# Bias rows, single weight loads, a second batch in plain fp32 and a new order in an attention and feed-forward block

## The chip, the cores and the metric

The kernel runs on one core of one Trainium2 chip. The core has five instruction streams that matter here: TensorE (PE, with its weight loads PEld), VectorE (DVE), ScalarE (ACT), GpSimd (POOL) and SyncE (SP), which issues most of the DMA transfers. The metric is the time of one execution on the device in microseconds, as the median of several runs. The profile is of one more execution, with times from the start of its span.

## The reference

For each of 16 batches of 512 tokens with 256 features, in fp32: linear attention with 16 heads of 16, a residual and a layernorm, then a feed-forward layer with ternary weights, a residual and a layernorm.

```
q, k, v = x @ Wq.T + bq, x @ Wk.T + bk, x @ Wv.T + bv       # by heads of 16
qe, ke  = exp(q - max(q)), exp(k - max(k))                    # max over the 16 of a head
kv      = ke.T @ v                                            # 16 x 16 of each head
y       = (qe @ kv) / (qe . sum(ke) + 1e-6)
x1      = layernorm(x + y @ Wo.T + bo)
Wt      = clip(round(W / (mean|W| + 1e-5)), -1, 1)            # for W1 and W2
out     = layernorm(x1 + relu(x1 @ Wt1.T + b1) @ Wt2.T + b2)
```

## The kernel before

**The work of a batch.** A batch is four tiles of 128 tokens. The stages, by the names of the steps (a number behind a name is the tile, the half or the chunk):

- `ldt`, `ldx` load x turned (features on partitions) and x as it is. `xt`, `xtl` split the turned x into a high part in the fp32r type and the low rest.
- `qk` (L680) multiplies a tile by the q and k weights, 512 columns, in three products per chunk of 128 features: high by high, high by low, low by high. Batch 0 uses plain fp32 instead (`qkF`, L670). `mxa` (L690) adds the bias from the tile `bqk`, which holds the same row in all partitions, `mxb` (L696) takes the maximum of each head, `mxs` (L700) subtracts it, `ex` (L711, L713) takes the exponential, for k a second time into fp32r.
- `ks`, `ksh`, `ksl`, `pks` (L758) sum exp(k) over the tokens. `dena` (L762), `denb`, `denc`, `nrm` (L790) divide exp(q) by its denominator, giving `qs`.
- `g` (L813, plain fp32 in batch 0: `gF`, L809) multiplies x by exp(k); `ge` copies it; `kv` (L840) multiplies it by the v weights `wv`; `kvm`, `kvb`, `kvp`, `kvh`, `kvl` mask and split it; `m` (L868) folds in the output weights.
- `qs` has to be turned. Batch 0 does it on TensorE (`qt`, L941, with `qteF` copying it out of PSUM). Batches 1 to 15 use a 32 x 32 transpose on VectorE (`qtr`, L898), a write to DRAM (`qtw`, L905), four reads back (`qtd`, L912), and `qtbe`, `qtbl` for the split.
- `o` (L1066, plain in batch 0: `oF`, L1062) gives the attention's output, `or` (L988) adds it to x. `xb` (L823) has added `bo` to x before. `nm`, `nq`, `nv`, `np`, `na` are the layernorm. `x1b` (L1081) adds `b2` for later.
- x1 is turned in the same two ways (`xt1...`): on TensorE in batches 0 and 15.
- `f` (L1098) is the first layer, eight chunks of 128 of the 1024 inner features, with `ha` (relu, L1104), `hc` and `hb` (the split of the result); `z` (L1135) is the second layer; `zr`, `ym`, `yq`, `yv`, `yp`, `ya` add, take the layernorm, and `st` stores. In the last batch the second layer is cut by tiles (`zL`) and each tile has its own layernorm, so that stores start early.

**The start.** `lqk0`, `lqk1` load the q and k weights in two halves of the features, by ACT's queue; `wh`, `wl` split them. `lbqk` loads the two biases into `bqk`, each read 128 times from DRAM, once per partition. `lw0` and `lw1` load the four pieces each of W1 and W2, `sa0` and `sa1` sum their absolute values, `tot`, `half` make the threshold, `qn` and `qz` (L580) make each piece ternary. `lvo` loads, one behind the other, `bv`, `wv`, `wo`, `bo` (repeated to all partitions), `b1` and `b2` (repeated). `warm0` and `warm1` are products of ones with ones on TensorE whose results nobody reads, twelve and two of them.

**The order.** No loop runs at build time in the order of the stages. A table `ORDER` gives each step of each batch a number, all steps are sorted by it, and each engine executes its own instructions strictly in that order. `OTHER` lists the steps and batches that use the second of two possible engines (for instance `mxs` on VectorE instead of GpSimd).

```
order = [(ORDER[name][0], 0, name, fn) for name, fn in startup_steps()]
for b in range(NB):
    order += [(ORDER[name][b], b, name, fn) for name, fn in steps(b)]
for _, b, name, fn in sorted(order, key=lambda e: e[0]):
    ...
```

So a step that waits holds up everything behind it on its engine, and a transfer that waits holds up everything behind it on SP. Buffers are few: two for the turned x (`xt32`), one for `ex`, two PSUM banks for each of four groups of uses (`qk` and the transposes; `g`, `kv`, `m`, `o`, `pks`; `f`; `z`). `GB` and `OB` say how many of the first batches use the plain form for `g` and for `o`; `MOVED` says which batches turn `qs` and x1 by way of DRAM; `WARM` holds the numbers of warm-up products.

Of the kernel before, what the change touches and what calls it, by code (L numbers as in the profile page):

```python
# [17 lines left out]
F32 = mybir.dt.float32  # L18
F32R = mybir.dt.float32r
AF = mybir.ActivationFunctionType  # L20
# [23 lines left out]
GB = 1  # L44
OB = 1
KB = 0
JB = 2
MOVED = {"qt": range(1, 16), "xt1": range(1, 15)}
WARM = (12, 2)
GROUPS = {"s": 2, ("y", 15): 4, ("s", 15): 4}  # L50
OTHER = {
    "xtl1": (1, 3, 7, 15),
    "qn2": (0,),
    "ks": (0, 1, 2, 4, 5, 8, 11),
    "ksl": (0, 1, 2, 3, 4, 5, 7, 8, 10, 11, 12, 13, 14, 15),
    "qn0": (0,),
    "xsl1": (1, 3, 12, 13),
    "qn1": (0,),
    "qn3": (0,),
    "mxs0": (1, 9, 10, 11, 12, 13, 14),  # L60
    "qn6": (0,),
    "nm0": (0, 1, 2, 3, 5, 7, 8, 9, 10, 11, 14),
    "ek0": (1, 3, 4, 8, 9, 10, 11, 12, 13, 14),
    "ek1": (1, 2, 3, 4, 6, 7, 8, 9, 11, 12, 13, 14, 15),
    "nv0": (0, 3, 8, 9, 13),
    "kvp": (1, 3, 4, 5, 7, 9, 12, 14, 15),
    "xb0": (1, 3, 7, 12, 15),
    "kvl": (1, 2, 3, 4, 5, 7, 8, 10, 11, 12, 13, 15),
    "xsl0": (2, 4),
    "xb1": (1, 3, 4, 13),  # L70
    "qn7": (0,),
    "qn4": (0,),
    "x1b1": (0, 6, 11),
    "qn5": (0,),
    "qtbl0": (2, 3, 4, 9, 15),
    "x1b0": (0, 1, 7, 9, 11, 12, 13),
    "xt1bl0": (1, 2, 3, 5, 7, 10, 14),
    "hc4": (1, 5, 6, 9, 14),
    "nrm0": (3, 7, 8, 9, 10, 11),
    "na0": (2, 6, 8, 14),  # L80
    "mxs1": (4, 7, 13, 14),
    "mxs2": (4, 7, 13, 14, 15),
    "xt1bl1": (2, 3, 4, 5, 6, 10, 12),
    "ym0": (1, 2, 5, 8),
    "na2": (3, 4, 15),
    "hc5": (2, 7, 13, 14, 15),
    "hc7": (2, 5, 10, 11, 12, 13, 15),
    "qtbl1": (4, 7, 15),
    "yv0": (2, 3, 4, 6, 11),
    "nrm1": (5, 11, 13, 14),  # L90
    "ya0": (2, 6, 7, 8, 12, 13, 15),
    "na1": (4, 7, 11, 14, 15),
    "mxs3": (7, 10, 13),
    "hc2": (4, 5, 6, 8, 11, 13, 14),
    "hc3": (4, 12, 13, 14),
    "ya3": (3, 6, 11, 12, 13),
    "hc6": (4, 8, 9),
    "xtl0": (10, 13),
    "hc1": (5, 7, 10, 11, 12, 15),
    "ya2": (4, 11, 13, 14, 15),  # L100
    "ya1": (5, 7, 11, 12, 13, 14),
    "hc0": (9, 10, 13, 14),
    "na3": (10, 13),
    "ym2": (15,),
    "yv1": (15,),
    "yv2": (15,),
    "ym3": (15,),
# [4 lines left out]
    "warm0": (2,),  # L112
    "wh0": (3,),
    "ldt0a": (4, 0, 0, 0, 0, 0, 0, 0, 0, 0, 0, 0, 0, 0, 0, 0),
    "qkF0_0": (5, 0, 0, 0, 0, 0, 0, 0, 0, 0, 0, 0, 0, 0, 0, 0),
    "wl0": (6,),
    "ldt1a": (7, 0, 0, 0, 0, 0, 0, 0, 0, 0, 0, 0, 0, 0, 0, 0),
    "wh1": (8,),
    "wl1": (9,),
    "lbqk": (10,),  # L120
    "qkF0_1": (11, 0, 0, 0, 0, 0, 0, 0, 0, 0, 0, 0, 0, 0, 0, 0),
    "mxa0": (12, 101, 119, 271, 362, 547, 589, 741, 927, 1135, 1172, 1344, 1546, 1661, 1766, 1938),
    "ldt0": (0, 13, 61, 158, 231, 346, 335, 545, 743, 893, 792, 1025, 1049, 1380, 1562, 1505),
    "xt0": (0, 14, 62, 177, 257, 386, 387, 643, 809, 894, 831, 1113, 1220, 1402, 1644, 1808),
    "mxb0": (15, 113, 120, 279, 365, 550, 598, 744, 932, 1169, 1173, 1345, 1547, 1662, 1783, 1976),
    "ldt1": (0, 16, 72, 108, 208, 221, 411, 416, 690, 915, 826, 1099, 1082, 1363, 1631, 1725),
    "xt1": (0, 17, 77, 117, 239, 344, 467, 630, 775, 916, 901, 1231, 1218, 1392, 1657, 1847),
    "xtl1": (0, 18, 94, 141, 248, 402, 516, 634, 817, 933, 1024, 1249, 1219, 1393, 1705, 1848),
    "qkF1_0": (19, 0, 0, 0, 0, 0, 0, 0, 0, 0, 0, 0, 0, 0, 0, 0),
    "ldt1b": (20, 0, 0, 0, 0, 0, 0, 0, 0, 0, 0, 0, 0, 0, 0, 0),  # L130
    "mxs0": (21, 115, 155, 306, 420, 551, 662, 784, 961, 1170, 1326, 1401, 1548, 1672, 1826, 2008),
    "exF0": (22, 0, 0, 0, 0, 0, 0, 0, 0, 0, 0, 0, 0, 0, 0, 0),
    "ldt0b": (23, 0, 0, 0, 0, 0, 0, 0, 0, 0, 0, 0, 0, 0, 0, 0),
    "xtl0": (0, 24, 69, 183, 278, 413, 521, 659, 816, 945, 975, 1296, 1351, 1403, 1666, 1814),
    "qkF1_1": (25, 0, 0, 0, 0, 0, 0, 0, 0, 0, 0, 0, 0, 0, 0, 0),
    "mxa1": (26, 88, 160, 232, 322, 474, 670, 765, 871, 1053, 1184, 1394, 1452, 1680, 1840, 1903),
    "mxb1": (27, 89, 164, 244, 323, 514, 712, 799, 889, 1067, 1281, 1408, 1453, 1681, 1841, 1914),
    "lw0": (28,),
    "sa0": (29,),
    "mxs1": (30, 114, 165, 280, 446, 515, 730, 840, 953, 1100, 1300, 1409, 1511, 1728, 1842, 1990),  # L140
    "exF1": (31, 0, 0, 0, 0, 0, 0, 0, 0, 0, 0, 0, 0, 0, 0, 0),
    "lvo": (32,),
    "woh": (33,),
    "qkF2_0": (34, 0, 0, 0, 0, 0, 0, 0, 0, 0, 0, 0, 0, 0, 0, 0),
    "qkF2_1": (35, 0, 0, 0, 0, 0, 0, 0, 0, 0, 0, 0, 0, 0, 0, 0),
    "mxa2": (36, 58, 162, 205, 444, 472, 625, 783, 973, 1045, 1294, 1333, 1561, 1599, 1732, 1942),
    "mxb2": (37, 59, 185, 302, 447, 541, 626, 791, 974, 1107, 1305, 1334, 1563, 1605, 1733, 2004),
    "ldx": (38, 70, 179, 154, 326, 524, 642, 845, 931, 1076, 1269, 1386, 1556, 1706, 1717, 1948),
    "mxs2": (39, 71, 186, 327, 448, 564, 692, 847, 985, 1144, 1329, 1404, 1580, 1614, 1734, 2055),
    "exF2": (40, 0, 0, 0, 0, 0, 0, 0, 0, 0, 0, 0, 0, 0, 0, 0),  # L150
    "qkF3_0": (41, 0, 0, 0, 0, 0, 0, 0, 0, 0, 0, 0, 0, 0, 0, 0),
    "qkF3_1": (42, 0, 0, 0, 0, 0, 0, 0, 0, 0, 0, 0, 0, 0, 0, 0),
    "mxa3": (43, 50, 189, 291, 397, 609, 717, 824, 850, 1087, 1239, 1423, 1494, 1578, 1739, 2018),
    "mxb3": (44, 96, 190, 292, 401, 610, 718, 825, 851, 1102, 1274, 1424, 1545, 1583, 1825, 2019),
    "mxs3": (45, 106, 206, 330, 423, 611, 742, 844, 1011, 1121, 1278, 1435, 1569, 1633, 1845, 2020),
    "exF3": (46, 0, 0, 0, 0, 0, 0, 0, 0, 0, 0, 0, 0, 0, 0, 0),
    "sr0": (47,),
    "qk3": (0, 48, 188, 270, 376, 562, 716, 732, 839, 1073, 1205, 1310, 1442, 1577, 1738, 2007),
    "tot0": (49,),
    "half0": (51,),  # L160
    "qn2": (52,),
    "qk2": (0, 53, 161, 204, 366, 460, 607, 780, 856, 997, 1191, 1297, 1462, 1595, 1731, 1917),
    "wol": (54,),
    "ks": (55, 124, 214, 371, 478, 640, 746, 863, 1058, 1200, 1347, 1482, 1584, 1747, 1901, 2076),
    "ksh": (56, 128, 215, 372, 502, 653, 757, 885, 1060, 1201, 1356, 1483, 1601, 1758, 1915, 2102),
    "bvm": (57,),
    "gF0": (60, 0, 0, 0, 0, 0, 0, 0, 0, 0, 0, 0, 0, 0, 0, 0),
    "warm1": (63,),
    "ksl": (64, 133, 227, 382, 503, 654, 758, 890, 1061, 1204, 1367, 1496, 1602, 1759, 1926, 2122),
    "pks": (65, 148, 228, 383, 530, 677, 769, 913, 1095, 1208, 1368, 1497, 1606, 1773, 1943, 2123),  # L170
    "dena": (66, 149, 238, 384, 531, 678, 771, 922, 1096, 1211, 1369, 1500, 1616, 1775, 1944, 2124),
# [1055 lines left out]
```

## Time and profile before

| | us |
|---|---|
| median of 3 runs (484.08 to 484.88) | 484.31 |
| the profiled execution, whole | 484.78 |
| the profiled execution, its span | 483.1 |
| TensorE busy | 469.2 |
| VectorE busy | 439.9 |
| ScalarE busy | 406.2 |
| GpSimd busy | 378.8 |
| first product of `f` of batch 0 starts at | 47.93 |
| last product of TensorE starts at | 476.94 |

A busy time is the time in which an engine executes an instruction; register and semaphore instructions do not count. Products are pipelined, so the distance from one start to the next says more than a product's own length: 24 products of 128x256 in 2.87 us are 0.12 us apart, though each is listed with 0.28. Where a line names two engines around an arrow, the second ended the wait of the first. SP shows only the issue of a transfer; its landing is later by some microseconds, which the part on DMA issues gives as a median per line.

### The profile page before, as it was taken

How to read it: one execution, taken by the hardware profiler on the slowest of the kernel's cores; microseconds unless marked ns; L12 is line 12 of the kernel's file. 1: busy time of each engine (PE TensorE's matmuls, PEld its weight loads, DVE VectorE, ACT ScalarE, POOL GpSimd, SP SyncE). 2: the span in 40 equal slices, each digit the busy share in tenths (PEclk: the TensorE clock that was granted, in tenths of full speed). 3: DMA queues.
4: the chain of work that ended last, by engine and by line, in shares of the span. 5: the costliest groups of instructions: out<-in, count | busy, mean ns of one | idle time of the engine just before them, and what ended most of it. 6: DMA issues, size and time to landing. Idle time of an engine off the chain costs nothing.

```text
span 483.1 us, 9025 instructions
## 1 busy us (share of the span) xinstructions
PE 469.2 (97%) x2976; PEld 415.9 (86%) x2976; DVE 439.9 (91%) x859; ACT 406.2 (84%) x923; POOL 378.8 (78%) x391
## 2 busy tenths in 40 slices
PE   8989999999999999999999999999999999999995
PEld 5567899899888998989989898889989898898984
DVE  2889999999999999999999998999999988998964
ACT  3897998998889788997987989688898979966774
POOL 1788898976958999896989799798898778744524
PEclk9999999999999999999999999999999999999999
DMA  6931325071542745345332605323445145124102
GB/s 227 309 140 43 89 88 196 24 229 55 160 125 68 216 143 153 104 127 175 130 133 87 199 22 188 118 99 121 152 130 148 51 156 150 44 89 132 44 1 88
DMA packets 36671, 59.84 MB, mean 124 GB/s; under 512 B 4240, under 2 KB 22672, under 8 KB 36624
## 3 DMA queue, kind: packets, MB, share of 16 engines
q1 hardware_dynamic: 36048, 58.74, 38.1%
q8 instruction: 23, 0.38, 0.3%
q10 hardware_dynamic: 576, 0.52, 0.3%
q14 instruction: 24, 0.20, 0.2%
HBM read 35.66 MB, written 23.59 MB: 123 GB/s over the span
## 4 chain that ended last, share of the span: by engine, by line
PE 79%; DVE 6%; POOL 5%; DMA 4%; ACT 3%; issue 2%; ACTq 0%; POOLq 0%; DVEq 0%
PE ph L1098 22%; PE pz L1135 21%; PE pqk L680 14%; PE po L1066 8%; PE pg L813 8%; PE pkv L840 2%; PE pm L868 2%; DMA w32qk<-in_wkT_dram 1%; DMA x<-in_x_dram 1%; POOL qk L700 1%; DMA w<-in_w1T_dram 1%; DVE x1b L1037 1%; PE pg L809 1%; PE pks L758 1%; POOL rstd_z L1020 1%
## 5 line engine op out<-in xcount | busy, mean ns | idle before, releaser
L1104 ACT ACTIVATE ph<-ph,b_sb 128x512 f32<-128x512 f32 x128 | 83.7, 657 | 20.9 <-PE ph L1098 19.9
L700 POOL TENSOR_TENSOR qk<-qk,mx 128x512 f32<-128x512 f32 x45 | 51.6, 1150 | 12.7 <-DVE mx L696 12.1
L690 DVE TENSOR_TENSOR qk<-pqk,bqk 128x512 f32<-128x512 f32 x64 | 43.2, 679 | 3.8 <-PE pqk L680 1.5
L696 DVE TENSOR_REDUCE mx<-qk 128x32 f32<-128x512 f32 x64 | 43.4, 679 | 1.2
L711 ACT ACTIVATE ex<-qk 128x512 f32<-128x512 f32 x64 | 40.4, 631 | 3.9 <-POOL qk L700 3.1
L790 POOL TENSOR_TENSOR qs<-ex,rden 128x512 f32<-128x512 f32 x22 | 26.2, 1204 | 13.2 <-DVE rden L782 13.1
L1005 ACT ACTIVATE junk_z<-x1b,nm_z 128x256 f32<-128x256 f32 x64 | 32.2, 505 | 2.4 <-POOL nm_z L999 2.2
L1035 ACT ACTIVATE x<-x,nmr_o,rstd_o 128x256 f32<-128x256 f32 x50 | 28.0, 600 | 7.3 <-POOL nmr_o L1022 7.3
L1005 ACT ACTIVATE junk_o<-x,nm_o 128x256 f32<-128x256 f32 x64 | 32.1, 503 | 0.4
L823 POOL TENSOR_TENSOR x<-x,bo_bc 128x512 f32<-128x512 f32 x23 | 30.6, 1335 | 0.1
L1081 POOL TENSOR_TENSOR x1b<-x,b_bc 128x512 f32<-128x512 f32 x22 | 29.5, 1346 | 1.4 <-ACT x L1035 1.4
L988 DVE SCALAR_TENSOR_TENSOR x1b<-pz,x1b 128x256 f32<-128x256 f32 x64 | 24.7, 417 | 1.7 <-PE pz L1135 1.5
L988 DVE SCALAR_TENSOR_TENSOR x<-po,x 128x256 f32<-128x256 f32 x64 | 24.3, 417 | 1.5 <-PE po L1066 1.0
L1035 ACT ACTIVATE x1b<-x1b,nmr_z,rstd_z 128x256 f32<-128x256 f32 x39 | 21.8, 598 | 4.2 <-POOL nmr_z L1022 4.2
L777 DVE TENSOR_REDUCE den<-dent 128x64 f32<-128x1088 f32 x16 | 20.5, 1281 | 0.2
L762 DVE TENSOR_TENSOR dent<-ex,pks 128x1024 f32<-128x1024 f32 x16 | 19.4, 1214 | 1.0 <-PE pks L758 1.0
L898 DVE STREAM_TRANSPOSE rqT<-qs 128x1024 f32<-128x1024 f32 x15 | 18.6, 1240 | 1.7 <-POOL qs L790 1.3
L1020 POOL TENSOR_TENSOR rstd_z<-var_z,expo 128x4 f32<-128x4 f32 (+1 forms) x19 | 19.2, 1011 | 1.0
L898 DVE STREAM_TRANSPOSE rx1T<-x 128x1024 f32<-128x1024 f32 x14 | 17.4, 1240 | 1.9 <-ACT x L1035 1.2
L1020 POOL TENSOR_TENSOR rstd_o<-var_o,expo 128x4 f32<-128x4 f32 x16 | 18.1, 1131 | 0.8
L840 PEld LDWEIGHTS pkv<-g,wv 128*128 128x128 f32 x128 | 16.2, 191 | 2.2 <-ACT g L832 1.3
L840 PE MATMUL pkv<-g,wv 128*128 128x128 f32 x128 | 17.0, 276 | 0.7 <-ACT g L832 0.7
(899 smaller groups left out, 2122.6 us busy)
## 6 DMA issues: line engine op xcount, KB each, us to landing
x<-in_x_dram SPq DMA_DIRECT2D x16, 512.0 KB, 4.5
xt<-in_xT_dram SPq DMA_DIRECT2D x30, 256.0 KB, 4.1
wqT<-rqT SPq DMA_DIRECT2D x15, 512.0 KB, 2.6
dqT<-wqT SPq DMA_DIRECT2D x60, 128.0 KB, 3.2
out_dram<-x1b SPq DMA_DIRECT2D x30, 256.0 KB, 2.2
wx1T<-rx1T SPq DMA_DIRECT2D x14, 512.0 KB, 2.6
dx1T<-wx1T SPq DMA_DIRECT2D x56, 128.0 KB, 3.2
w<-in_w1T_dram SPq DMA_DIRECT2D x4, 256.0 KB, 4.2
```

The costliest lines, as they stand in the source:

```text
L680: nc.tensor.matmul(s.pqk[t], s.xt[i][:, c, tt], wqk[j][:, c, :], start=(c == 0 and n == 0), stop=(c == EC - 1 and n == 2))
L690: nc.vector.tensor_tensor(s.qk[t].rearrange("p g d -> p (g d)"), s.pqk[t], bqk, ALU.add)
L696: nc.vector.tensor_reduce(s.mx[t], s.qk[t], AX.X, ALU.max)
L700: engine(f"mxs{t}", b, nc.gpsimd, nc.vector).tensor_tensor(s.qk[t], s.qk[t], s.mx[t].unsqueeze(2).to_broadcast([P, 2 * NH, HD]), ALU.subtract)
L840: nc.tensor.matmul(s.pkv[:, cc], wv[:, ec, cc], s.g[:, ec, cc], start=(ec == 0), stop=(ec == EC - 1))
L988: nc.vector.scalar_tensor_tensor(out=r, in0=p[t], scalar=1.0, in1=r, op0=ALU.mult, op1=ALU.add, accum_out=stat("sum")[:, t:t + 1])
L1005: nc.scalar.activation(junk, getattr(s, what)[:, t, :], AF.Square, bias=n.nm[:, t:t + 1], accum_out=stat("sq")[:, t:t + 1])
L1020: nc.gpsimd.tensor_tensor(stat("rstd")[:, sl], n.var[:, sl], expo[:, sl], ALU.pow)
L1035: nc.scalar.activation(r, r, AF.Identity, bias=nmr, scale=rstd)
L1098: nc.tensor.matmul(s.ph[f], w1[:, c, f * P:(f + 1) * P], s.x1T[i][:, c, :], start=(n == 0), stop=(n == 2 * EC - 1))
L1104: nc.scalar.activation(s.ph[f], s.ph[f], AF.Relu, bias=b1_sb[:, f:f + 1])
L1135: nc.tensor.matmul(s.pz[t], hx[:, t * P:(t + 1) * P], w2[:, f, :], start=(done[tt] == 1 and t == tt[0] and i == 0), stop=(done[tt] == FC a ...
```

## The change

Four things change together.

1. The biases of q and k are loaded as one row each, 1 KB, into partition 0 of `bqk`, which is cleared before. `pbqk` multiplies a 128x128 tile of ones by it on TensorE, which puts the row into all partitions of a PSUM bank of the `qk` group, and `bqke` copies it back to `bqk` on ScalarE.
2. `lvo`, `lw0`, `lw1`, `sa0`, `sa1` are cut into steps of one instruction each (`lbv`, `lwv`, `lwo`, `lbo`, `lb1`, `lb2`, `lw0_0` to `lw1_3`, `sa0_0` to `sa1_3`), so each has its own place in the order.
3. Batch 1 uses the plain fp32 form for `g` and `o` (`GB = 2`, `OB = 2`) and turns `qs` on TensorE (`MOVED`). With that it has no `xs`, `xsl`, second exponential of k, `ek`, `qtr`, `qtw`, `qtd`, `qtbe`, `qtbl` and `ml`.
4. `ORDER` and `OTHER` are new in all their numbers, for all batches, and `WARM` is (9, 2).

```
-GB = 1
-OB = 1
+GB = 2
+OB = 2
-MOVED = {"qt": range(1, 16), "xt1": range(1, 15)}
-WARM = (12, 2)
+MOVED = {"qt": range(2, 16), "xt1": range(1, 15)}
+WARM = (9, 2)
...
+    nc.vector.memset(bqk, 0.0)
...
         @step("lbqk")
         def _():
             for j, bias in enumerate((bq, bk)):
-                nc.sync.dma_start(out=bqk[:, j * E:(j + 1) * E], in_=bias.partition_broadcast(P))
-        @step("lvo")
-        def _():
-            nc.sync.dma_start(out=bv_col, in_=bv)
...
+                nc.sync.dma_start(out=bqk[0:1, j * E:(j + 1) * E], in_=bias.unsqueeze(0))
+        @step("pbqk")
+        def _():
+            halves["b"] = bank("pqk", [P, 512], "pbqk")
+            nc.tensor.matmul(halves["b"], ones, bqk, start=True, stop=True)
+        @step("bqke")
+        def _():
+            nc.scalar.copy(bqk, halves["b"])
+        def load_step(name, dst, src):
+            @step(name)
+            def _():
+                nc.sync.dma_start(out=dst, in_=src)
+        load_step("lbv", bv_col, bv)
+        load_step("lwv", wv, wvT.rearrange("(c p) o -> p c o", p=P))
...
-            @step(f"lw{j}")
+                @step(f"lw{j}_{q}")
...
+                @step(f"sa{j}_{q}")
...
```

The order of the first transfers, before and after, as the two tables give it (a number behind a point is the batch; `lqk` on ACT's queue, the rest on SP's):

```
before: lqk0 lqk1 | ldt0a.0 ldt1a.0 lbqk ldt0.1 ldt1.1 ldt1b.0 ldt0b.0 lw0 lvo ldx.0 ldt0.2 ldx.1 ldt1.2 lw1 ldt1.3 ldx.3 ldt0.3 ldx.2
after:  lqk0 lqk1 | lbqk ldt0a.0 ldt1a.0 ldt1.1 ldt0.1 ldt0b.0 lw0_0 ldt1b.0 lw0_2 lw0_3 lbv lw0_1 lw1_2 lwo lw1_0 ldt0.2 lw1_3 ldx.0
        ldt1.2 lw1_1 ldt1.3 ldx.2 ldt0.3 lwv ldt1.4 lbo ldt0.4 ldx.1 ldt0.5 lb2 ldx.3 lb1
```

TensorE's order up to the first products of `f`, in the same way:

```
before: warm0 qkF0 qkF1 qkF2 qkF3 (each in two halves) qk3.1 tot0 qk2.1 gF0.0 warm1 pks.0 gF1.0 kv.0 qk1.1 qk0.1 tot1 qt0.0 qt1.0 m.0
        qk0.2 oF0.0 oF1.0 pks.1 qk1.2 qk2.2 g0.1 g1.1 xt11.0 xt10.0 kv.1 qk3.2 f0.0 f3.0
after:  warm0 pbqk qkF0 qkF1 qkF2 qkF3 (each in two halves) qk3.1 qk1.1 tot0 qk2.1 gF0.0 pks.0 gF1.0 qk0.1 kv.0 tot1 qt0.0 qt1.0 m.0
        qk1.2 oF0.0 oF1.0 qk0.2 warm1 pks.1 qk2.2 gF0.1 gF1.1 qt1.1 qt0.1 xt11.0 xt10.0 kv.1 qk3.2 f4.0 f0.0
```

## The prediction

> **What bounds the kernel now.** I read the page's first part, then busy time by stretches, then the chain in order of time, then the timeline of the first 23 us, of f7 of batch 0 and of the end.
>
> The page, busy time and the chain's engines:
>
> ```profile
> PE 469.2 (97%) x2976; PEld 415.9 (86%) x2976; DVE 439.9 (91%) x859; ACT 406.2 (84%) x923; POOL 378.8 (78%) x391
> ...
> PE 79%; DVE 6%; POOL 5%; DMA 4%; ACT 3%; issue 2%; ACTq 0%; POOLq 0%; DVEq 0%
> ```
>
> TensorE is the bound, VectorE close behind. Where TensorE is not full, the stretches tell (columns: from:to, length, then busy us and instructions of PE, PEld, DVE, ACT, POOL, clock, DMA share, GB/s):
>
> ```profile
> 0.00:22.27 22.27, 18.95 (x69) 13.11 (x70) 12.26 (x27) 12.71 (x26) 9.19 (x17) 1.00 0.80 260
> 22.27:71.54 49.27, 46.70 (x270) 39.54 (x268) 47.19 (x87) 44.50 (x99) 43.04 (x40) 1.00 0.31 100
> ...
> 48.00:140.00 92.00, 92.00 (x594) 82.73 (x593) 87.04 (x162) 83.53 (x184) 75.76 (x73) 1.00 0.42 127
> 140.00:310.00 170.00, 168.15 (x1086) 150.63 (x1085) 162.01 (x310) 147.83 (x339) 152.69 (x149) 1.00 0.42 132
> 310.00:475.00 165.00, 164.75 (x1091) 148.86 (x1090) 151.35 (x309) 136.54 (x312) 115.57 (x125) 1.00 0.30 97
> ```
>
> From 48 to 475 TensorE loses about 2 of 427 us. The loss lies at the start. Before 22.27 us the "busy" 18.95 us holds 5.5 us of warm-up products and slow ones; from 22.27 to 71.54 VectorE is the full engine (47.19 of 49.27).
>
> The timeline of the start:
>
> ```profile
> 1.10 5.49 PE L466 MATMUL pwarm<-ones 128*128 128x128 f32 x24 [1.10 <-DVE eps L435]
> 1.70 0.42 SPq L496 DMA_DIRECT2D bqk<-in_bq_dram  x1
> 2.17 0.43 SPq L496 DMA_DIRECT2D bqk<-in_bk_dram  x1
> 6.39 1.46 PE L670 MATMUL pqk<-w32qk,xt 128*128 128x512 f32 x2
> 9.10 6.25 PE L670 MATMUL pqk<-w32qk,xt 128*128 128x512 f32 x14 [1.26 <-DMA xt<-in_xT_dram]
> 10.31 0.68 DVE L690 TENSOR_TENSOR qk<-pqk,bqk 128x512 f32<-128x512 f32 x1
> 12.97 0.33 SPq L640 DMA_DIRECT2D x<-in_x_dram  x1
> 19.58 1.97 PE L809 MATMUL pg<-ex,x 128*128 128x256 f32 x8 [0.72 <-DMA x<-in_x_dram]
> 22.27 1.22 DVE L762 TENSOR_TENSOR dent<-ex,pks 128x1024 f32<-128x1024 f32 x1 [0.62 <-PE pks L758]
> ```
>
> The second half of the q/k weights and x set the pace until 22 us. The DMA issues give 5.0 and 6.4 us to landing for the two bias broadcasts. They are in flight together with the weights that TensorE waits for until 9.1.
>
> **The costs of the parts.** Step lengths below are the means of their rows. An engine's steps overlap a little: VectorE's add up to 51.6 us between 22.27 and 71.54 where the profile shows 47.19 busy, a factor 0.915.
>
> *Plain fp32 in batch 1, on TensorE.* The chain in order of time has both kinds:
>
> ```profile
> 22.23 1.74 PE pg L809 x8
> ...
> 57.87 2.87 PE pg L813 x24
> 60.73 2.88 PE po L1066 x24
> ```
>
> The plain form takes 1.74 us for half a batch, so 3.48, against 2.87 for three split products: +0.6 for g and +0.6 for o. Eight transposes by TensorE at 0.11 us each: +0.9. The row that turns x1 gives that pitch (8 in the stretch 44.20 to 45.27, with the next product behind them). The Trainium skill, page "FP8 and Floating Point Precision", section "TensorE Precision Notes", says that true fp32 takes four passes, which against three split products speaks against this edit. By that rule alone it would cost a third of 2.87 twice, 1.9 us as an estimate, and the sum below would be 0.7 worse; the rows (3.48 against 2.87) are what is used.
>
> *The same, elsewhere.* Batch 1 loses xs (ACT 1.03), two xsl (0.63 on DVE and 1.28 on POOL), four second exponentials (4 x 0.41, ACT), two ek (POOL 3.0), qtr (DVE 1.24), ml (0.69, DVE), two qtbl (POOL 2.6); two copies from PSUM take the place of two from SBUF. SP loses qtw and four qtd transfers of batch 1, so nothing queues there behind a wait for qtr. That is 2.6 us of DVE, 2.7 of ACT, 6.9 of POOL, and the DVE part counts, since DVE is full there.
>
> *The bias row.* Two 1 KB loads replace two broadcasts of 128 KB. Added: a clearing of bqk on DVE (four times the 0.17 us of the 128x128 one at most; the loads on SP and perhaps the first warm-up product wait for it, +0.4), one fp32 product 128x512 (like a qkF: 6.25 us for 14 records, two records each, so 0.9 us), one ACT copy (0.59). The product's price has two ends: 0.9 at the later rate, and 1.7 if it runs at the slow rate of the first products (warm-up: 24 in 5.49 us, 0.21 apart, while the four at 21.38 take 0.61 us together). It stands just behind the warm-up, now 9 x 2 records, so I take 1.7 for the start and 0.9 for the sum of work. The Trainium skill, "TensorE: Matmul & The Clock Gate", Part 1, puts such a change of rate down to a gate that opens after some 3.4 us of activity, counted in windows that run freely; by that the product may fall on either side, 0.9 or 1.7. The granted clock of the stretches above reads 1.00 throughout, so here the pitch alone shows it.
>
> Sum of TensorE work: +1.2 +0.9 +0.9 = +3.0, less nothing for the warm-up, which fills idle time.
>
> *The start, step by step.* The weights share the first 8 transfers with 258 KB instead of 512 KB; the two halves and xt are 768 KB, and the stretch 0 to 5 us moved 153 GB/s, 765 KB. So the second half of the weights should land near 5.5 instead of 9.0. PE: warm-up from 1.5 to 5.5, bias to 7.2, the two qkF of the first tile to 8.8 (first mxa 10.31 before), the other six, 0.86 each, to 13.9. There stands a queue: on SP the xt load of batch 2 (`ldt0`) is now ahead of x of batch 0 (`ldx`), and must wait for the buffer that the last qkF reads. So x is issued near 14.8, not 12.97, with 4.5 us (the median row) lands at 19.3, as before. Meanwhile TensorE has three qk steps of batch 1 (1.4 each) ahead of gF0 instead of two. VectorE, from 8.8, has 12.5 us of steps up to the first dena (11.1 before, from 10.31 to 22.27): dena starts near 21.3, 1.0 earlier.
>
> *From there VectorE sets the time.* Before, from dena to the end of hb2 of batch 0 (71.54) it takes 75 steps, 51.6 us of row lengths; f7 starts right on it at 71.6, with 56.7 us of TensorE work done. In the new order the like point is f6, with 57.0 us done; it needs hb1, and that is 71 steps and 47.0 us behind dena. 47.0 x 0.915 + the same 2.1 idle = 45.1, so f6 at 66.4: 5.2 earlier. ACT's list to these points is shorter too (55.0 against 58.9 us), and POOL loses the 6.9. I add 0.5 for VectorE waiting on oF0 of batch 0, which comes behind nrm0, itself now behind kvp on POOL (bounds: -0.5, because POOL is emptier, to +2.6, a whole kv and nrm0).
>
> *The rest.* TensorE work behind that point: +3.0 -0.3 = +2.7. The single-step loads by themselves: no bytes change, the bo, b1 and b2 loads move behind x and w1; hidden by the 20 us until their first use; without that cover the broadcast costs its 4.7 us of landing. Moves of work between engines after batch 1: DVE -8 us over 13 batches (steps that went to ACT and POOL, POOL lighter in all): nothing, as TensorE covers them; bounds -2 (all that 48:475 loses) to +2 (as much again).
>
> *The end.*
>
> ```profile
> 476.94 0.28 PE L1135 MATMUL pz<-w,h_7l 128*128 128x256 f32 x1
> ...
> 477.65 0.42 DVE L988 SCALAR_TENSOR_TENSOR x1b<-pz,x1b 128x256 f32<-128x256 f32 x1
> ...
> 479.90 0.41 DVE L1031 TENSOR_SCALAR x1b<-x1b,nm_z,rstd_z 128x256 f32<-128x256 f32 x1 [0.74 <-POOL rstd_z L1020]
> ```
>
> Now tile 3 ends last; in the new order tile 2 does, whose steps need the product nmr (0.19 on POOL) and stand on ACT behind the square of tile 3 (0.51 and 0.19): 0.9 at most, less 0.3 for the add that no longer waits on DVE: +0.4.
>
> Sum on the profiled span: -5.2 +0.5 +2.7 +0.4 = -1.6 (483.1 to 481.5). The profiled execution took 484.78 in all, 0.5 over the median 484.31; against the median: 484.3 - 1.6 = 482.7.
>
> **Rivals.**
> 1. *The start gains less (no change).* If x lands 6.7 us after its issue, the median of the four x loads in the first 26 us, that is 21.5, and pks, dena and all behind come 2.2 later: -1.6 +2.2 = +0.6, 484.9. For: x was ready only at 19.45 before, though issued earlier. Against: SP's wait empties the queues ahead of it.
> 2. *Slower: wv comes late.* Its load moves from place 18 of the SP and ACT loads to place 29, behind x. kv of batch 0 needs it near 23.6. Eight transfers are in flight at a time (the ninth is issued when the first lands), so if each takes 7.1 us, as the w2 loads did, wv is issued when ldt0 of batch 2 lands (21.0) and lands at 28.1: 4.5 late, -1.6 +4.5 = +2.9, 487.2. Against: from 15 us on 2.6 MB lie ahead of its end, at the 379 GB/s of the stretch 20 to 25 us 6.8 us, so 22. It decides against the change from a landing later than 25.2.
> 3. *The parts gain, the order does not.* If VectorE's list were no help and only DVE's 2.6 us of batch 1 went, -2.6 +3.0 +0.4 = +0.8: 485.1. For: TensorE is full from 48 us on, so each gain must be made before.
>
> **How the numbers follow.** A measurement can tell about 0.2%, 1.0 us. Forecast case 0.50 (own range 480.5 to 483.8; 0.45 faster, 0.05 same). Rival 1: 0.17 (0.02 faster, 0.10 same, 0.05 slower). Rival 2: 0.18 (0.01 faster, 0.02 same, 0.15 slower). Rival 3: 0.15 (0.02 faster, 0.05 same, 0.08 slower). Faster 0.50, same 0.22, slower 0.28. Range 480.3 (the forecast with POOL's -0.5 and -2 in the middle, rounded) to 487.0, which takes in rivals 1 and 3 and half of rival 2.
>
> **What would show it.** Right: first mxa near 8.8, weights landed before 6, dena before 21.6, f6 of batch 0 near 66.9 with TensorE full from then on; the two oF of batch 1 near 1.75 us each. Wrong: TensorE waiting for wv at kv of batch 0; SP idle ahead of ldx beyond 14; idle TensorE between 70 and 470 above 4 us; an end over 6.5 us behind the last product.

## The result, and the profile after

| | before | after |
|---|---|---|
| median | 484.60 (4 runs, 484.08 to 484.88) | 490.73 (4 runs, 489.63 to 492.71) |
| ratio, 95% interval | | 1.013 (1.0095 to 1.017) |
| profiled execution, its span | 483.1 | 491.0 |
| last product of TensorE starts at | 476.94 | 484.25 |

The change made the kernel 6.1 us slower. The forecast was 482.7, a gain of 1.6 us, with a range up to 487.0. The profiled execution is the slowest of the four (492.71; the fastest took 489.63), so the losses read from it add up to some 2 us more than those of a median run.

The page of the changed kernel, busy time and the engines of the chain that ended last:

```profile
PE 472.7 (96%) x2964; PEld 418.0 (85%) x2964; DVE 445.0 (91%) x858; ACT 404.5 (82%) x923; POOL 365.3 (74%) x381
...
PE 48%; DVE 16%; POOL 9%; ACT 7%; issue 3%; DMA 2%; SPq 1%; POOLq 0%; DVEq 0%; ACTq 0%
```

TensorE has 3.5 us more busy time, VectorE 5.1. More telling is the chain: TensorE's share fell from 79% to 48%. For half of the span something else decided when the kernel went on. Where that is, the stretches tell (from:to, length, then busy us and instructions of PE, PEld, DVE, ACT, POOL, clock, DMA share, GB/s):

```profile
20.92:67.20 46.28, 44.69 (x242) 37.68 (x241) 44.84 (x83) 41.00 (x88) 35.85 (x35) 1.00 0.21 67
72.00:160.00 88.00, 85.40 (x553) 76.36 (x552) 82.81 (x160) 73.97 (x172) 70.74 (x71) 1.00 0.39 123
160.00:192.00 32.00, 26.77 (x161) 23.38 (x161) 27.43 (x51) 19.74 (x44) 23.45 (x23) 0.95 0.44 142
192.00:310.00 118.00, 117.76 (x766) 106.16 (x765) 111.64 (x215) 104.67 (x244) 98.73 (x97) 1.00 0.39 123
310.00:475.00 165.00, 164.30 (x1092) 148.64 (x1090) 151.50 (x300) 139.05 (x319) 116.56 (x125) 1.00 0.34 108
```

Between 160 and 192 us TensorE is busy for 26.77 of 32 us, at a granted clock of 0.95, and all four engines are below their share of the whole span. From 72 to 160 it lacks 2.6 us more. Behind 192 it is full.

A finer account takes the distances between the starts of neighbouring products, and for each line and shape the median distance as its work; what goes beyond is lost.

| us of TensorE | before | after |
|---|---|---|
| work (sum of median distances) | 460.9 | 463.7 |
| lost up to 70 us | 7.8 | 3.7 |
| lost from 70 to 130 | 0.5 | 2.9 |
| lost from 130 to 160 | 1.5 | 1.2 |
| lost from 160 to 192 | 0.2 | 7.6 |
| lost behind 192 | 4.9 | 3.9 |
| from the last product's start to the end | 6.1 | 6.7 |

The differences add up to +7.8, the spans differ by 7.9. The start came nearly as forecast, as its timeline shows:

```profile
5.10 1.29 PE L521 MATMUL pbqk<-bqk,ones 128*128 128x512 f32 x2
6.50 6.68 PE L708 MATMUL pqk<-w32qk,xt 128*128 128x512 f32 x15
8.55 0.69 DVE L728 TENSOR_TENSOR qk<-pqk,bqk 128x512 f32<-128x512 f32 x1 [0.38 <-ACT xt_1h L665]
11.79 0.34 SPq L678 DMA_DIRECT2D x<-in_x_dram  x1
15.85 0.40 SPq L530 DMA_DIRECT2D wv<-in_wvT_dram  x1
18.34 1.89 PE L847 MATMUL pg<-ex,x 128*128 128x256 f32 x8
23.57 1.13 PE L878 MATMUL pkv<-g,wv 128*128 128x128 f32 x8
```

The first add of the bias is at 8.55 (10.31 before), the first `g` product at 18.34 (19.58), and `kv` starts at 23.57 without a wait for `wv`. Then the place where the change lost most. The chain of waits in order of time (start, us, what), from GpSimd's remainder of the turned q of batch 5 to TensorE's expansion products of batch 4:

```profile
164.42 2.51 POOL qT_5l L971 x2
...
166.95 0.32 SPq L950
...
168.26 4.38 DMA dx1T<-wx1T
...
173.26 0.62 ACT x1T_4h L966
...
173.91 1.34 DVE x1T_4l L971
175.25 0.35 DVE x L1026 x2
...
175.65 1.52 PE pkv L878 x8
177.16 1.72 PE ph L1136 x4
```

The return transfers of x1 of batch 4 are issued right behind a GpSimd step that has nothing to do with x1. The waits of SP between 150 and 195 us name it (us in total, times, longest):

```profile
SPq L950 <- DMA wx1T<-rx1T: 4.4, 2, 2.3
SPq L950 <- DMA wqT<-rqT: 3.8, 2, 2.4
SPq L950 <- POOL qT_5l L971: 3.5, 1, 3.5
```

The first two are waits of a return for its own write, which are due; the third is not. The data land at 172.6, ScalarE and VectorE wait for them, and on VectorE the remainder `x1T_4l` stands ahead of two adds of `o` (L1026) that would free the PSUM bank that `kv` needs. So TensorE stands idle from 172.4 to 175.6, waiting for the bank of `kv`.

Why SP waits there is in the table of the order. Both turning paths share two buffers, `tr`, for the transposed tensor before it is written to DRAM and for the returned one. Which of the two buffers a tensor gets follows from the sequence of the steps.

```
            qtr.5  xt1r.4  qtd.5  xt1d.4        buffer of xt1d.4 becomes free with
before:      708     737     760    789          the write of x1 itself
            qtr.5  qtd.5   xt1r.4 xt1d.4
after:       720     746     763    765          the last remainder of q of batch 5 (step 801, GpSimd)
```

Before, the two transposed tensors come first and the two returns after them, so the return of x1 takes the buffer that its own write has just left. In the new order it takes the one in which the returned q of batch 5 still lies. The crossing alone is not new: in the built program of the kernel before, 8 returns take a buffer in which the other path's returned tensor lay, in the changed one 9. It costs time where the last reader is late: here GpSimd finishes q of batch 5 at 166.93, 6.15 us after x1 was sent to DRAM (160.78). Of the other crossings only the next one, the return of q of batch 6, shows a wait of SP over 0.4 us for a remainder of the other path, of 1.0 us.

### The profile page after: what moved, and what is told of

Same layout as the page of the kernel before. It is cut to its first block, busy times and chain, and to the rows that moved or that the text cites. A ratio compares the mean times of both kernels' runs of the same rounds, so it can differ in the third digit from the quotient of the medians.

```text
span 491.0 us, 8983 instructions
## 1 busy us (share of the span) xinstructions
PE 472.7 (96%) x2964; PEld 418.0 (85%) x2964; DVE 445.0 (91%) x858; ACT 404.5 (82%) x923; POOL 365.3 (74%) x381
## 4 chain that ended last, share of the span: by engine, by line
PE 48%; DVE 16%; POOL 9%; ACT 7%; issue 3%; DMA 2%; SPq 1%; POOLq 0%; DVEq 0%; ACTq 0%
PE pz L1173 15%; PE ph L1136 14%; PE pqk L718 6%; PE pg L851 5%; PE po L1104 5%; DMA dx1T<-wx1T 1%; PE pkv L878 1%; ACT ph L1142 1%; DVE x1b L1026 1%; DVE x L1026 1%; POOL qs L828 1%; DVE mx L734 1%; POOL qk L738 1%; ACT junk_z L1043 1%; PE pm L906 1%
## 5 line engine op out<-in xcount | busy, mean ns | idle before, releaser
L738 POOL TENSOR_TENSOR qk<-qk,mx 128x512 f32<-128x512 f32 x48 | 52.7, 1103 | 8.4 <-DVE mx L734 8.2
L1026 DVE SCALAR_TENSOR_TENSOR x1b<-pz,x1b 128x256 f32<-128x256 f32 x64 | 24.2, 417 | 7.6 <-PE pz L1173 6.0
L1073 ACT ACTIVATE x<-x,nmr_o,rstd_o 128x256 f32<-128x256 f32 x47 | 26.4, 596 | 4.4 <-POOL nmr_o L1060 4.0
L1026 DVE SCALAR_TENSOR_TENSOR x<-po,x 128x256 f32<-128x256 f32 x64 | 24.4, 417 | 0.5 <-PE po L1100 0.2
L1058 POOL TENSOR_TENSOR rstd_z<-var_z,expo 128x4 f32<-128x4 f32 (+1 forms) x19 | 18.1, 956 | 8.5 <-ACT var_z L1052 7.7
L1073 ACT ACTIVATE x1b<-x1b,nmr_z,rstd_z 128x256 f32<-128x256 f32 x37 | 20.6, 596 | 2.0 <-POOL nmr_z L1060 2.0
L772 POOL TENSOR_TENSOR ks<-ex 128x512 f32<-128x512 f32 x11 | 15.1, 1369 | 7.2 <-ACT ex L749 7.1
L936 DVE STREAM_TRANSPOSE rqT<-qs 128x1024 f32<-128x1024 f32 x14 | 17.3, 1239 | 1.6 <-POOL qs L828 1.3
```

The lines of the kernel that those rows point to most:

```text
L738: engine(f"mxs{t}", b, nc.gpsimd, nc.vector).tensor_tensor(s.qk[t], s.qk[t], s.mx[t].unsqueeze(2).to_broadcast([P, 2 * NH, HD]), ALU.subtract)
L1026: nc.vector.scalar_tensor_tensor(out=r, in0=p[t], scalar=1.0, in1=r, op0=ALU.mult, op1=ALU.add, accum_out=stat("sum")[:, t:t + 1])
L1058: nc.gpsimd.tensor_tensor(stat("rstd")[:, sl], n.var[:, sl], expo[:, sl], ALU.pow)
L1073: nc.scalar.activation(r, r, AF.Identity, bias=nmr, scale=rstd)
```

## The experiments

All are complete kernels. Line numbers of the rows shown are up to one higher than the changed kernel's. The kernel before was run again beside them, with a median of 484.27 for e1 to e4, 484.67 for e5 to e8, 484.62 for e9 to e11 and 484.34 for e12; each ratio is to its own.

### The parts, the start and the middle, one at a time

Four kernels put the change together from its pieces. An engine order can be cut: the first steps of one table, then the remaining steps in the sequence of the other.

```
 parts, GB, OB, bias row, single loads:
+  as in the changed kernel, in all four
 ORDER and OTHER:
   e1_parts       before's, each new step in the place of its old one (WARM 12, 2)
   e2_newstart    the changed kernel's through f7 of batch 0 (340 steps), then before's
   e3_newmiddle   before's through f7 of batch 0, then the changed kernel's (WARM 12, 2)
   e4_oldengines  ORDER the changed kernel's, OTHER from batch 2 on before's
```

> The new parts in the old order: bias row with its product with ones, weight loads in single steps and the second batch in plain fp32, each in the place that its old step had; old engines, old warm-up count. Theory A (the new order of the middle loses the time, in waits of TensorE between 70 and 190 us): the parts only add TensorE work, +3.0 us, less what the start gains, so 484 to 487 us. Rival B (the parts themselves cost it, the plain fp32 batch above all): 489 to 492 us, the time of the changed kernel. Rival C (bias row late): a start later than 10.3 us for the first add of the bias.

> All parts of the change; the changed kernel's order and engines up to the last expansion product of batch 0 (near 71 us), and from there the order and engines of the kernel before. Theory A: the start keeps its gain of some 4.5 us, TensorE has 2.8 us more work and the middle does not wait, 484.6 - 4.5 + 2.8 = 482.9, with up to 2 for the seam: 482 to 485 us. Rival B (the parts): 489 us or more. Rival D (TensorE is merely earlier after the new start, so any order behind it runs into VectorE, ScalarE and GpSimd, which had no lead to give): 487 to 490 us, with TensorE waiting 5 us or more between 70 and 190 us here too.

> All parts of the change; the old order and engines up to the last expansion product of batch 0 (near 71 us), and from there the order and engines of the changed kernel. Theory A: the middle waits here too and the start gains nothing: 490 to 496 us. Rival D (it is the early start that the others cannot follow): the later start gives them their lead back, TensorE waits under 3 us between 70 and 190 us, 485 to 488 us.

> The changed kernel in its own order, but from the third batch on each step on the engine that it had before. Theory A1 (the order itself makes the waits): 488 to 494 us, TensorE waiting near 175 us as in the changed kernel. Rival A2 (the new choice of engines makes them, VectorE with 5 us more work): 483 to 486 us, TensorE waiting under 2 us between 70 and 190 us.

| | median | ratio to before, 95% |
|---|---|---|
| e1_parts | 488.02 | 1.0075 (1.0058 to 1.0091) |
| e2_newstart | 484.26 | 0.9998 (0.9987 to 1.0009) |
| e3_newmiddle | 498.14 | 1.030 (1.028 to 1.032) |
| e4_oldengines | 564.96 | 1.166 (1.164 to 1.168) |

From 130 to 192 us the kernel before has this stretch:

```profile
130.00:192.00 62.00, 61.01 (x393) 54.75 (x392) 58.17 (x118) 53.16 (x119) 52.86 (x54) 1.00 0.47 143
```

The stretches of the kernel with the new start and the old middle:

```profile
72.00:100.00 28.00, 27.04 (x180) 24.42 (x180) 25.27 (x50) 22.36 (x52) 21.08 (x20) 1.00 0.32 110
...
130.00:192.00 62.00, 61.04 (x396) 54.88 (x394) 58.28 (x118) 53.50 (x120) 52.83 (x54) 1.00 0.45 143
```

and of the one with the old start and the new middle:

```profile
72.00:100.00 28.00, 23.91 (x142) 20.89 (x142) 23.22 (x42) 20.23 (x47) 22.25 (x20) 0.94 0.33 96
...
130.00:192.00 62.00, 59.38 (x377) 53.56 (x376) 57.63 (x107) 49.30 (x116) 47.79 (x49) 0.97 0.38 120
```

With the old order behind it the new start leaves TensorE full from 130 to 192 (61.04 of 62, as before: 61.01); with the new order behind the old start it waits again, SP with the same 3.5 us for the turned q of batch 5. So theory A holds in what it says of the cause: it is the order of the middle that waits. Its ranges held only for e2_newstart: e3_newmiddle lies 2.1 us above its 490 to 496, with a wait of TensorE of 2.5 us at 78 us for a weight piece that the changed kernel has with 1.1, and e1_parts lies 1.0 above its 484 to 487. Rival D, that any order behind an early start would wait, falls on both runs. Rival B is half right: the parts in the old order cost 3.7 us. Rival C falls, the first add of the bias is at 8.98 in e1_parts. The change in steps by medians: 484.3, +3.7 for the parts, -3.8 for the new order of the start (484.26 - 488.02), +6.5 for the new order of the middle (490.73 - 484.26). The six runs of e1_parts lie between 486.95 and 489.06, so the first two terms are sure to about 1 us only.

The fourth run misses both expectations by far. The new order with the old choice of engines takes 564.96 us: TensorE is busy for 89% of the span, VectorE, ScalarE and GpSimd for 82, 71 and 65%. No engine is full; they wait for each other. The new order rests on its own choice of engines from batch 2 on. The old order with the new choice was not run.

### The shared buffer

```
-TB = 2
+TB = 3
-JB = 2
+JB = 1
-den = small.tile([P, T * NH], F32, tag="den", ...)
+den = small.tile([P, T * NH], F32, tag="den", ..., bufs=1)
```

> The changed kernel with a third buffer for the turned tensors (tr), paid for by one junk buffer and two den buffers less, which only their own engine writes and reads in turn. Theory E (the stall at 175 us hangs on the shared buffer: the return transfers of x1 of batch 4 stand on SyncE behind GpSimd's remainder of the turned q of batch 5, 3.5 us): they go out when their write has landed, TensorE's 3.4 us at 175.65 and the slow products behind it go, and the change's time falls by 3.5 to 6 us, to 485 to 487 us. Rival F (VectorE, ScalarE and GpSimd are simply behind there, and the buffer is one of several waits of the same length): the stall falls by under 1.5 us, or as much comes back within the next 30 us, 488.5 to 491 us.

That took away the wait at 175 us (lost between 160 and 192: 1.5 us instead of 7.6), but the median was 489.13, only 1.6 under the changed kernel, and 7.1 us were lost behind 192 instead of 3.9. By what was written down, rival F had it. But the second line of the edit was not free: with one junk buffer ScalarE's squares that follow each other start 0.635 us apart instead of 0.503 (medians), and its busy time rose from 404.5 to 410.2. So the same was done without it, with space from elsewhere:

```
-TB = 2
+TB = 3
-ones = const.tile([P, P], F32, ...)
+ones = as32(onesr)                   # the tile that the row sums use
-den, rden in three buffers
+den in one, rden in two
```

> The changed kernel with the third buffer for the turned tensors, now with both junk buffers kept (the space comes from the ones, which are read from the tile that the row sums use, and from den and rden). Theory E (the 6 us lost between 160 and 192 us hang on that buffer): TensorE loses under 2 us there instead of 7.6, nothing comes back later, 484.5 to 486.5 us. Rival F2 (without that stall the same lag shows in other waits): over 2 us come back behind 192 us as in the first run with three buffers, 488 to 489.5 us.

Median 486.17, ratio to before 1.003 (1.002 to 1.004): 4.6 us under the changed kernel. SP's transfers of batch 4's x1 go out 4.1 us earlier, first in the changed kernel, then with the third buffer:

```profile
160.78 0.34 SPq L943 DMA_DIRECT2D wx1T<-rx1T  x1
166.95 1.74 SPq L950 DMA_DIRECT2D dx1T<-wx1T  x4
```

```profile
159.74 0.34 SPq L944 DMA_DIRECT2D wx1T<-rx1T  x1
162.85 1.74 SPq L951 DMA_DIRECT2D dx1T<-wx1T  x4
```

The stretches with the third buffer:

```profile
160.00:192.00 32.00, 31.02 (x204) 28.05 (x204) 31.61 (x67) 24.48 (x57) 29.45 (x27) 1.00 0.49 163
192.00:280.00 88.00, 87.79 (x573) 79.39 (x571) 82.47 (x157) 77.99 (x179) 71.38 (x71) 1.00 0.43 139
```

From the write of x1 to its return it is 3.1 us instead of 6.2. TensorE does 31.02 us of 32 between 160 and 192, and behind that nothing comes back (4.0 us lost against 3.9). Theory E holds, and rival F2 falls: one buffer, shared by two paths, makes 4.6 of the 6.5 us of the new middle, by medians of runs that spread over 3.1 and 1.9 us. For the other 1.9 us the trace shows where they are lost, not what would mend them: TensorE loses 2.1 us between 70 and 130 us here, 1.4 in e2_newstart, and 1.4 between 160 and 192, against 0.1.

### The slow products behind the wait

In the changed kernel the first expansion products behind TensorE's idle stretch (172.4 to 175.6) stand 0.43 us apart instead of 0.23. This run puts work there that computes nothing: it adds products of zeros into the open sum of `z` of batch 3.

```
+zeros = const.tile([P, P], F32R, ...)      # 0.0 * ones
...
+if (b, f) == (3, 4):
+    for _ in range(28):
+        nc.tensor.matmul(s.pz[0], zeros, w2[:, f, :], start=False, stop=False)
```

> The changed kernel with 28 products of zeros, added into the open sum of z of batch 3 in the place where TensorE stands idle for 3.4 us near 175 us (28 x 0.117 = 3.3 us of work, nothing is computed by them). Theory G (an idle TensorE of that length slows the products behind it): the eight products of the next expansion run at 0.23 us apart instead of 0.43, and the time falls by 1 to 1.5 us against the changed kernel, 489 to 490 us. Rival H (the slow products have another cause): they stay at 0.43, 490.5 to 492 us.

Median 488.47, 2.3 us under the changed kernel, though TensorE has 3.3 us more to do. The stretches, first of the changed kernel:

```profile
172.50:175.60 3.10, 0.00 (x0) 0.00 (x0) 1.69 (x4) 1.98 (x4) 2.17 (x2) 1.00 0.17 70
175.60:179.50 3.90, 3.85 (x14) 3.30 (x15) 3.58 (x8) 1.89 (x7) 2.41 (x3) 0.59 0.74 195
```

and of this run:

```profile
172.50:175.60 3.10, 3.10 (x29) 3.10 (x28) 3.10 (x7) 1.79 (x6) 3.10 (x3) 1.00 0.19 48
175.60:179.50 3.90, 3.90 (x28) 3.54 (x27) 3.29 (x7) 2.60 (x9) 1.67 (x2) 1.00 0.87 237
```

The granted clock behind the idle stretch is 0.59 in the one and 1.00 in the other, and the eight expansion products stand 0.23 us apart here (175.94 to 177.65). Theory G holds. The run gave more than expected; in its trace the 0.9 us wait at 186.8 is gone as well.

### Where the start's gain comes from, and what plain fp32 is worth

```
 e7_start_plain: ORDER, OTHER
+  the changed kernel's for its first 98 steps (to about 24 us), then before's
 e8_start_split: the same, and
-GB = 2
-OB = 2
+GB = 1
+OB = 1        # batch 1 in split products, qs turned by way of DRAM, as before
```

> Only the first 98 steps (to about 24 us) in the changed kernel's order, all behind them in the order and engines of the kernel before, with the plain fp32 second batch. Theory A: the start's gain of some 4 us stays, 3 us of work more, no wait at 73 us for the weight pieces: 483 to 485 us. Rival I (the gain needs the changed kernel's order up to 70 us): 486 to 488 us, as the parts alone in the old order.

> As the run before it in the list, but the second batch in split products as in the kernel before. Theory J (TensorE is the bound, so its 2.8 us of work are what the plain batch costs): 2 to 3 us under the run with the plain batch, 480.5 to 482.5 us, and faster than both kernels. Rival K (VectorE sets the time until 70 us, and the plain batch spares it 2.6 us): within 1 us of the run with the plain batch.

485.82 (ratio 1.003, 1.002 to 1.004) and 487.97 (1.007, 1.005 to 1.009). The first lies between its two expectations. By medians the first 98 steps bring 2.2 of the 3.8 us between e1_parts and e2_newstart. TensorE's account says otherwise: up to 70 us it loses 7.8 us in the kernel before, 6.5 in e1_parts, 6.7 here and 3.8 in e2_newstart, so the drop comes from the steps behind the first 98. With the spread of e1_parts the share stays open.

The second went against both: less work for TensorE made the kernel 2.2 us slower. TensorE waits 2.2 us at 28.1 and 1.6 at 30.1, and works at the low clock behind that (0.50 from 30.2 to 34). The stretch 20 to 46, plain first, then split:

```profile
20.00:46.00 26.00, 23.10 (x122) 19.17 (x121) 23.53 (x45) 21.78 (x49) 18.83 (x17) 1.00 0.26 91
```

```profile
20.00:46.00 26.00, 20.54 (x103) 17.12 (x102) 21.30 (x40) 19.17 (x44) 18.04 (x16) 0.87 0.26 95
```

VectorE is less busy with the split batch than without (21.30 against 23.53 us), so it is not short of time. The waits between 24 and 40 us name what is late (in total, times, longest):

```profile
POOL xs_1l L691 <- ACT xs_1h L685: 3.4, 1, 3.4
DVE xs_1l L691 <- ACT xs_1h L685: 2.0, 1, 2.0
PE tot L593 <- DVE kvm L885: 2.0, 1, 2.0
PE pqT L980 <- POOL qs L829: 1.5, 1, 1.5
```

The split of x of batch 1 (`xs`) comes on ScalarE only at 26.07, behind steps for the weight pieces. Its remainders stand on VectorE ahead of `kvm` and on GpSimd ahead of `qs` of batch 0, so both engines stand idle and hold those up, and TensorE with them. So the plain batch pays behind this start because it takes these steps out of the queues; not shown is that it would pay with `xs` at another place, nor that VectorE's 2.6 us are what it spares. Neither theory J nor rival K foresaw this.

### Single steps put earlier

The waits that remain are each for one VectorE step. Three runs move such steps.

```
 e10_mended (changed kernel, third buffer):       e11_newstart_moved (new start, old middle):
+  qz5 ahead of hb6.0                            +  qz5 ahead of hb6.0
+  hb4.1 ahead of or2.2                          +  f5.3 ahead of o1.4
+  hb4.2 ahead of ek0.5                          +  hb7.8 ahead of kvb.11
+  hb1.4 ahead of na3.5
                                                  e12_two_moves (new start, old middle):
                                                 +  hb7.8 ahead of kvb.11
                                                 +  ks.5 behind ml.4 (ksh.5, ksl.5 later)
```

> As the run before it in the list, and four VectorE steps put ahead of one neighbour each, where TensorE waited for them: the sixth weight piece (73 us), the remainder of h_4 of batch 1 (88 us) and of batch 2 (134 us), and that of h_1 of batch 4 (184 to 189 us). Theory L (VectorE has the time, only its sequence is wrong there, 1.1 + 1.1 + 0.8 + 1.1 us): 3 to 4 us under the run before it, 481 to 483 us. Rival M (VectorE is full from 20 to 190 us, so what is put back becomes late next): under 1.5 us of gain.

> The new start up to 71 us with the old order behind it, as in the run of that kind, and three steps moved by one place or a few: the sixth weight piece ahead of a remainder (73 us), an expansion product of batch 3 ahead of the two o products of batch 4 (142 us), the last remainder of batch 8 ahead of a small VectorE step of batch 11 (308 us). TensorE loses 1.1 us at each of the three now. Theory L: 0.7 + 0.9 + 0.6 = 2.2 us less, 482 us, faster than both kernels. Rival M: under 1 us of gain, 483.5 to 484.5 us.

> The new start with the old order behind it, and two local moves of VectorE steps away from the weight pieces: the last remainder of batch 8 ahead of a small step of batch 11 (308 us), and the folding sums of k of batch 5 behind the remainder of m of batch 4 (142 us; the two steps that read them go two places down on ScalarE and GpSimd). TensorE loses 1.0 and 1.1 us there in the run without the moves. Theory L (sequence only): the 308 us wait falls to 0.3 and the 142 us wait to under 0.3 us, 484.26 - 1.7 = 482.6, faster than both kernels. Rival M (VectorE is full near 142 us): the second wait comes back within 15 us at another place, 483.3 to 484.3 us.

488.26 (1.008, 1.007 to 1.010), 484.94 (1.001, 1.000 to 1.002) and 484.11 (1.000, 0.999 to 1.001). The move at 308 us did what was expected: TensorE's loss between 280 and 370 fell from 1.7 to 0.4 us in the second run and to 0.5 in the third. In the first run the wait at 133 us went, too (the loss from 130 to 160 fell from 1.3 to 0.5). But what these gave was lost elsewhere: between 70 and 130 us TensorE lost 4.5 us instead of 2.1 in the first run, which is 2.1 us slower than the run with the third buffer alone, and 3.1 instead of 1.4 in the second; between 130 and 160 it lost 2.3 instead of 1.5 in the third. That is what rival M says, though it did not foresee a loss. The traces show one way in which a moved step becomes late again. The sixth weight piece (`w`, L619), where it stood and where it was put, each with the GpSimd step beside it. In the run without the move:

```profile
72.42 1.49 DVE L619 SCALAR_TENSOR_TENSOR w<-w,half,neg 128x512 fp32r<-128x512 f32 x2
70.17 2.53 POOL L739 TENSOR_TENSOR qk<-qk,mx 128x512 f32<-128x512 f32 x2
```

and with it:

```profile
71.43 1.41 DVE L619 SCALAR_TENSOR_TENSOR w<-w,half,neg 128x512 fp32r<-128x512 f32 x1
69.76 2.52 POOL L739 TENSOR_TENSOR qk<-qk,mx 128x512 f32<-128x512 f32 x2
```

Two pieces took 1.49 us; the moved one alone takes 1.41. It starts inside GpSimd's step, which ends at 72.28, and ends 0.56 us behind that. TensorE's wait at 73 us kept its 1.1 us. In the last run the same met the remainder of the turned q, which the move had put 1.4 us earlier:

```profile
137.95 1.78 DVE L972 TENSOR_TENSOR qT_4l<-dqT,qT_4h 128x512 fp32r<-128x512 f32 x1
137.63 1.56 POOL L670 TENSOR_TENSOR xt_7l<-xt,xt_7h 128x512 fp32r<-128x512 f32 x1 [2.76 <-ACT xt_7h L666]
```

That step took 0.68 us where it stood before. No version was found that beats both kernels: the new start with the old middle (484.26) and the last one (484.11) equal the kernel before within the noise.

## Why the prediction was wrong, point by point

**What bounds the kernel.** Right for the kernel before. In the changed start VectorE is again the fullest engine, 44.84 of 46.28 us up to f6 of batch 0. That its amount of work sets the time there is not shown apart; e8_start_split was slower by waits for ScalarE's `xs`.

**Plain fp32 and the sum of TensorE's work.** By the median distances the plain `g` and `o` cost +1.2 and the transposes +0.9, both as forecast, and the bias product 1.4 instead of 0.9. The table's +2.8 is near the forecast +3.0 partly by luck: it also holds the six warm-up records fewer, -1.3, and +0.5 from a median distance of 0.233 instead of 0.232 us for `f`. The two `oF` of batch 1 take 1.89 us each as listed, 1.73 by the distance of their starts. The Trainium skill ("FP8 and Floating Point Precision", section "TensorE Precision Notes") gives true fp32 four passes; taken as passes of equal length that would be a third more than three split products. Here it is less: the 16 records of plain `g` of batch 1 are 0.216 us apart, 3.46 us, and 24 split products 0.12 us apart, 2.88.

**The bias product.** Taken at 1.7 at the start, measured 1.29 as listed, between the two ends.

**The start.** First add of the bias 8.8 against 8.55, `dena` 21.3 against 20.92, f6 of batch 0 near 66.9 against 67.2. That f6 starts 4.4 us before the like point 71.6; forecast were 4.7. TensorE's loss up to 70 us fell by 4.1, where the forecast takes 5.0 (4.7 and the 0.3 us more of work done). The sign and nearly the size were right, though two details were not: ScalarE could take the weights only at 6.22 and not near 5.5, and x was issued at 11.79 and not near 14.8, as SP waited only 0.4 us for the buffer. The row of the kernel before also puts TensorE's wait until 9.10 down to the turned x, and not to the weights; ScalarE took the second half of these at 9.04, so both came at about the same time.

**Rivals 1 and 2.** x did not land late, and `wv`, issued at 15.85, kept no one waiting. Both fall.

**"The rest", the new order behind the start: "nothing, as TensorE covers them; bounds -2 (all that 48:475 loses) to +2 (as much again)".** This is the step that failed: the term for new waits in the middle was put at nothing, and it measured +6.5 us by medians (490.73 against 484.26 of e2_newstart). Between 70 and 192 us TensorE lost 11.7 us instead of 2.2 in the profiled execution. It went wrong in three ways.

- The bound of +2 was taken from what TensorE had lost there before. That says how well the old order kept it fed, and nothing of a new one. e3_newmiddle and e4_oldengines show how wide the true range was: an order, or a choice of engines, can cost 14 or 80 us over the kernel before with the changed kernel's parts.
- The queues that the steps were moved past were not followed. The turned x1 of batch 4 came behind a buffer that q of batch 5 still held; the four numbers of the table above say so, and SP's 3.5 us wait is worth 4.6 us (e9_third_buffer_alone).
- "VectorE -8 us over 13 batches" is a sum over stages that do not lie together, and it leaves out batches 0 and 15. The same count of steps by row means, cut at batch 7, gives +4.3 for batches 2 to 6 and -12.5 for 7 to 14, and the new waits lie in the first part. Batches 0 and 15 gain some 7 us, so that VectorE has 858 steps after 859. Its busy time did not fall: it rose from 439.9 to 445.0. Its 128x512 steps that took over 0.9 us, counted with what they took beyond 0.70, make 8.3 us before and 13.4 after, as much as the rise.

**Rival 3, that the order gives nothing**, stood at 485.1. e1_parts is this case, and took 488.02: the parts in the old order cost more than the +0.8 of its sum. That the new order itself makes new waits was not among the rivals. It should have been: with every number of a long table new, it was a likely way to lose.

**The end.** +0.4 forecast, +0.6 measured.

**The range.** Its low end, 480.3, does not come out of its own terms: 482.7 with -0.5 in place of +0.5 and with -2 gives 479.7. Nothing rests on it.

**The signs named.** One of the four that would show it wrong came clearly: over 4 us of idle TensorE between 70 and 470. The end, at 6.7 us behind the last product's start, just passed the 6.5 named.

Leaving the middle out, the forecast was -2.0 for parts and start together; e2_newstart measured 0.0 by medians, -0.5 by the profiled spans. About 1 us of the difference is the start, which saved 4.0 us of TensorE's losses and not 5.0; about 0.9 is the loss between 70 and 130 us, with the 1.1 us wait at 73 us for the sixth weight piece.

## What to carry to other kernels

An order written out step by step is a set of buffers as much as a set of queues. Before an order is costed, list for each tile with few buffers who takes which one, who frees it and when. Two paths can share a pair of buffers without loss, as most crossings here show; they lose where a transfer gets the buffer whose last reader stands late in another engine's queue. And a bound for a new order is not read from how little the old one lost: when all numbers change, let the range run far to the slow side.

A sum of work by engine is read by stage, and a step that is put earlier is costed with what the neighbouring engine does at its new time.

## What the runs showed of the hardware

**A short idle stretch lowers TensorE's clock afterwards.** In the changed kernel it was 3.3 us of idle and a granted clock of 0.59 in the 3.9 us behind it; with the stretch filled (e6_fill) it was 1.00. In e3_newmiddle a wait of 2.5 us was enough, and the slow part came late:

```profile
78.00:81.00 3.00, 0.49 (x3) 0.11 (x2) 2.08 (x4) 1.43 (x3) 3.00 (x3) 1.00 0.75 233
81.00:83.00 2.00, 2.00 (x15) 2.00 (x16) 1.46 (x1) 0.00 (x0) 2.00 (x2) 0.81 1.10 263
83.00:85.00 2.00, 2.00 (x11) 2.00 (x11) 0.00 (x0) 1.58 (x4) 1.40 (x2) 0.50 0.84 236
85.00:87.00 2.00, 2.00 (x17) 2.00 (x16) 1.79 (x3) 2.00 (x5) 1.24 (x1) 0.84 0.42 159
```

TensorE starts again at 80.92 at full rate, falls to half near 82.2 and is back at 85.6: some 3.4 us at half rate, 1.7 us lost on top of the wait. The Trainium skill, "TensorE: Matmul & The Clock Gate", Part 1, gives one idle window of about 3.4 us as the cause, in windows that run freely. The length of the slow part and its late start agree with such windows; that 2.5 us of idle were enough does not agree with a wholly idle one.

**VectorE waits for GpSimd's whole step.** A VectorE step with two inputs from SBUF that starts inside a GpSimd step takes as long as GpSimd still needs, and 0.55 us more: 1.41, 1.78, and in the changed kernel, where both halves of one remainder are released together, 1.80 instead of 0.68:

```profile
131.68 1.80 DVE L757 TENSOR_TENSOR exk_5l<-ex,exk_5h 128x512 fp32r<-128x512 f32 x1
131.64 1.29 POOL L757 TENSOR_TENSOR exk_5l<-ex,exk_5h 128x512 fp32r<-128x512 f32 x1
```

Counted over the profiles for steps of 128x512 on both engines, 25 of VectorE's 99 such steps start inside a GpSimd step in the kernel before, and all end 0.54 to 0.60 us behind it. In the changed kernel it is 36 of 102, and 35 end 0.54 to 0.66 us behind it; the other starts 0.02 us after the GpSimd step and keeps 0.67 us, and the GpSimd step takes 1.86. Steps that read PSUM, such as the 128 remainders of `h`, keep 0.63 to 0.69 whatever GpSimd does. The Trainium skill, "SBUF — State Buffer", section "SBUF: two separate sides", says just this: the port pair of the two is locked for a whole instruction, by a VectorE operation with two SBUF inputs against a GpSimd one that reads SBUF. The trace agrees with it. The row means used for the forecast (0.69 for most such steps) hold such waits only as far as the old order met them.

**One junk buffer instead of two** for the squares, whose result nobody reads, cost about 3 us (489.13 against 486.17), with 4.5 us more of ScalarE's busy time over 128 squares (410.2 against 405.7). The two kernels also differ in where ones, den and rden lie, so this is not shown apart.
